# Two attention stages in one hand-ordered pipeline: the masked slots of batches 1 to 7 stand three slots later

## The chip, the cores and the metric

The kernel runs on one core of one Trainium2 chip. The metric is the device time of one execution in microseconds (us). Three runs of the kernel before gave 2798.55, 2795.04 and 2800.26 us; the median is 2798.55 us.

The engines are PE (TensorE, matmul, with its weight loads PEld), DVE (VectorE), ACT (ScalarE), POOL (GpSimd) and SP (SyncE, which issues the transfers). Each runs its own list of instructions in the order in which the kernel wrote them, and an instruction that must wait holds up what stands behind it in that list.

## The reference

`x` is 8 batches of 256 channels by 512 tokens. Four layers follow, each with a residual:

```
x = x + masked_attention(x, mask=cond)          # 8 heads of 32, keys == queries == values
x = x + modulated_attention(x, cond, ...)       # rms norm, scale and shift, 16 heads of 32, rms norm of q and k
x = x + scan_RK4(cond, drive=x)                 # 256 steps, one after another
x = x + scan_GRU(cond, inputs=x)                # 256 steps, one after another
```

Everything is float32. Only the two attention layers are touched by the change. In the masked attention, the logits of a row are `(scores * cmask + (1 - cmask) * -1e30) * rmask`, softmax over the keys, and then a 256x256 output projection. In the modulated attention, `x` is normalised per channel row, scaled and shifted by vectors made from `cond`, projected to q, k and v (512 to 1536), and attended over 256 rows in 16 heads of 32; the result is `o + o @ W_out`.

## The kernel before, in words

The function `attention` writes both attention layers for all batches as one software pipeline. Its loop `for g in range(-5, ...)` (L501) runs over **slots**; in each slot it writes a piece of several batches, in an order set by hand (`tc.manual_schedule()`, L500). Nothing reorders the instructions afterwards. A slot is only a place in this order: it has no fixed length, and lasts as long as its work and its waits.

**Masked attention of a batch** takes eight units, one for each of two groups of four heads (`e` = 0, 1) and each of four blocks of 128 keys (`kc` = 0 to 3). I write a unit as (b,e,kc). Relative to the batch's base slot, `U*b` with `U = 8`, they stand as follows.

- `load` (seven slots ahead), `project` and `mask` (L193, L208; rel. -5 and -4): the projection and its masked copy; `project_out` (L212) turns it for the values one slot later.
- `scores0` (L218; rel. -4 to 3): one unit's scores, 8 matmuls on PE into four PSUM banks, and four copies out by ACT. Then `maxima0` (L232), a 128x2048 reduction on DVE.
- `rows0` (L238; after a group's fourth maximum): PE transposes the maxima, ACT copies them (`mrow`), and two steps of transfers spread them over all partitions (`row`, then `bc`).
- `weights0` (L250; rel. 1 to 8): DVE subtracts `bc` from the unit; `exps0` (L254): ACT takes its exponential.
- `values0` (L258; rel. 2 to 9): PE sums values and weights, 16 matmuls.
- `weigh0` (L275; with a group's last `values0`): two reciprocals and two products on DVE, then two passes on POOL that make `ctxT`.
- `masked_out` (L289; rel. 10): the output projection on PE, added to `x` by DVE.

**Modulated attention of a batch**:

- `normalize` (L302; slot `norms[b]`): two squares on ACT with their sums, two tiny powers on POOL, two scaled copies `xh` on ACT. `modulate` (L314), a slot later: eight transposes and four ACT copies to `xnT`.
- `qkv` (L329), six parts, from two slots after `norms[b]` (three for batch 6), one to a slot and two to a slot for the last two batches; for q and k, `qkv_norm` (L352) on DVE and POOL and `qkv_out` (L366) a slot later.
- From `HEADS[b]` on, four groups of heads: `maxima1` (PE, DVE), `rows1`, `weights1` (PE, then ACT exponentials), `values1` (PE, DVE), one group to a slot, staggered.
- `modulated_out` (L438), in two halves, at the slots `OUT[b]`.

The order inside a slot has two forms. In a slot that is `late` (a group of heads of batch 0 to 5 is under way), `exps0` and `values0` stand at the end of the slot, and a `weigh0` that falls due is written only in the next slot, behind that slot's `maxima1` and `values1` (`due`, L513). In other slots, `values0` stands near the front and `weigh0` follows in the same slot.

PSUM gives one ring of five banks to scores, projections, transposes and outputs (`bank`, L61), used in turn, and single banks `c0`, `c1` to the two sums of `values0` and `c2` to `values1`.

In the steady state, `masked_out` of batch b stands in the slot after its last `weigh0`'s slot, and `normalize` of b one slot after `masked_out`. Behind the last output the two scans run for the rest of the span.

Of the kernel before, what the change touches and what calls it, by code (L numbers as in the profile page):

```python
# [16 lines left out]
B, T, D = 8, 256, 512  # L17
# [8 lines left out]
def attention(ctx, tc, cst, x, cond, wqT, woT, w_emb, b_emb, g_norm, w_qkv, g_q, g_k, w_out, follow):  # L26
# [21 lines left out]
    U = 8  # L48
# [12 lines left out]
    def bank(shape, name):  # L61
        return ps_s.tile(shape, F32, tag="s", name=name)
# [149 lines left out]
    def project_out(b, e, qt):  # L212
        pt = bank([P, NJ, P], f"ptq_{b}_{e}")
        for c in range(NJ):
            nc.tensor.transpose(pt[:, c, :], qt[:, c * P : (c + 1) * P], ident)
        nc.scalar.copy(qtoks[b][:, :, e * P : (e + 1) * P], pt)
# [21 lines left out]
    def rows0(b, e):  # L238

        pt = bank([P, P], f"pm0_{b}_{e}")  # L240
        nc.tensor.transpose(pt, mxp0, ident)
        mrow = ftwo.tile([P, P], F32, tag="mrow", name=f"mrow0_{b}_{e}", bufs=1)
        nc.scalar.copy(mrow, pt)
        bc = bcs[b, e] = ftwo.tile([P, 4, D], F32, tag="bc", name=f"bc_{b}_{e}")
        row = dram.tile([4, D], F32, tag="row", name=f"row_{b}_{e}", bufs=2)
        for h in range(4):
            nc.sync.dma_start(row[h].rearrange("(q n) -> q n", n=P), mrow[32 * h : 32 * h + 4, :])
        nc.sync.dma_start(bc, row.rearrange("h n -> (h n)").partition_broadcast(P).rearrange("p (h n) -> p h n", h=4))
# [126 lines left out]
    def maxima1(b, c):  # L375
        qT, kT = qTs[b], kTs[b]

        ss = []
        for h in range(4):
            n = f"n1_{b}_{c}_{h}"  # L380
            ss.append(other_bank([P, 2, 256], f"c{h}", n) if b == B - 1 and h < 2 else bank([P, 2, 256], n))
        for qc in range(2):
            for h in range(4):
                r = 32 * h
                nc.tensor.matmul(  # L385
                    ss[h][:, qc, :],
                    lhsT=qT[r : r + 32, c, qc * P : (qc + 1) * P],
                    rhs=kT[r : r + 32, c, :],
                    start=True,
                    stop=True,  # L390
                )
        for h in range(4):
            nc.vector.tensor_reduce(mxp1[:, 32 * h : 32 * h + 2], ss[h], AX.X, ALU.max)  # L393
# [36 lines left out]
    def values1(b, c):  # L430
        if c == 0:
            oTs[b] = big.tile([P, NJ, 256], F32, tag="oT", name=f"oT_{b}")
        pc = other_bank([P, 2, 256], "c2", f"pc1_{b}_{c}")
        for half in range(2):
            values(pc, half, lambda k, h: vts[b][:, k, c * P + h * DH : c * P + (h + 1) * DH], [exs1[b, c]])
        weigh(pc, oTs[b][:, c, :], f"1_{b}_{c}")
# [32 lines left out]
    PARTS = ((2, 0), (2, 1), (1, 0), (1, 1), (0, 0), (0, 1))  # L469


    norms, parts, HEADS, OUT = [], {}, [], []
    for b in range(B):
        per = 2 if b >= B - 2 else 1
        norms.append(U * b + U + (2 if b == B - 1 else 3))
        start = norms[b] + (2 if b != B - 2 else 3)
        for i, part in enumerate(PARTS):
            parts.setdefault(start + i // per, []).append((b, *part))
        HEADS.append(start + len(PARTS) // per)
        OUT.append((HEADS[b] + 6, HEADS[b] + (8 if per == 1 else 7 if b < B - 1 else 6)))  # L480

    def at(g, rel, n=1):

        b, r = divmod(g - rel, U)
        return (b, r) if 0 <= b < B and r < n else None

    def heads(g, rel, which=range(B)):

        for b in which:
            if 0 <= g - HEADS[b] - rel < NJ:  # L490
                return b, g - HEADS[b] - rel
        return None
# [3 lines left out]
    def leave(kind):  # L496
        for key in [k for k in left if k[0] == kind]:
            yield *key[1:], left.pop(key)

    with tc.manual_schedule():  # L500
        for g in range(-5, OUT[-1][1] + 1):  # L501

            a0, v0 = at(g, -4, U), at(g, 2, U)
            w1, v1 = heads(g, 1), heads(g, 2)

            a1, early = heads(g, 1, range(B - 2)), heads(g, 0, range(B - 2, B))
            late = a1 is not None or heads(g, 0, range(B - 2)) is not None
            turns, turned = list(leave("qkv")), list(leave("qt"))
            if a1:
                maxima1(*a1)  # L510
                if v1:
                    values1(*v1)
                if a := due.pop("weigh", None):  # L513
                    weigh0(*a)
            elif a0:
                scores0(a0[0], a0[1] // 4, a0[1] % 4)
            if (a := at(g, -3, U)) and a[1] % 4 == 3 and g > 0 and not a1:
                rows0(a[0], a[1] // 4)

            pr = at(g, -5, 2)  # L520
            if pr and not late:
                project(*pr)
            if v0 and not late:
                values0(v0[0], v0[1] // 4, v0[1] % 4)
            for a in turned:
                project_out(*a)
            if g == OUT[-1][1]:
                cst["soon"]()
                scan_start(cst["pool"], nc, cst)
            if g - 1 in norms:  # L530
                modulate(norms.index(g - 1))
            if a1 and a0:
                scores0(a0[0], a0[1] // 4, a0[1] % 4)
            if (a := at(g, -3, U)) and a[1] % 4 == 3 and a1:
                rows0(a[0], a[1] // 4)
            if w1:
                rows1(*w1)
            if e0 := at(g, 1, U):
                weights0(e0[0], e0[1] // 4, e0[1] % 4)
                if not late:  # L540
                    exps0(e0[0], e0[1] // 4, e0[1] % 4)
            if pr and not late:
                mask(*pr)
            if v0 and not late and v0[1] % 4 == 3:
                weigh0(v0[0], v0[1] // 4)
            if a0 and a0[1] % 4 < 3:
                maxima0(a0[0], a0[1] // 4, a0[1] % 4)

            if pr and late:
                project(*pr)  # L550
                mask(*pr)
            if a := at(g, U + 2):
                masked_out(a[0])
            if 3 <= g < 7:
                modulation(2 * g - 6)
            if g == U:
                scale_shift()
                add_identity()
            if g in norms:
                normalize(norms.index(g))  # L560
            made = [(part, qkv(*part)) for part in parts.get(g, ())]
            for b in range(B):
                for half in range(2):
                    if OUT[b][half] == g:
                        modulated_out(b, half)
                    if OUT[b][half] == g and (b, half) == (B - 1, 0):
                        for s in range(4):
                            for m in range(NJ // 2):
                                drive_of(nc, cst["us"], cst["x2T"], cst["ubias"], 0, s, m)
            if a0 and a0[1] % 4 == 3:  # L570
                maxima0(a0[0], a0[1] // 4, 3)
            if g == -1:
                rows0(0, 0)
            for part, lines in made:
                if lines:
                    qkv_norm(*part, *lines)
                    left["qkv", *part] = lines[1]
            if not w1:
                for a in turns:
                    qkv_out(*a)  # L580
            if early:
                maxima1(*early)

            if v1 and not a1:
                values1(*v1)
            if w1:
                weights1(*w1)
                for a in turns:
                    qkv_out(*a)
            if e0 and late:  # L590
                exps0(e0[0], e0[1] // 4, e0[1] % 4)
            if v0 and late:
                values0(v0[0], v0[1] // 4, v0[1] % 4)
                if v0[1] % 4 == 3:
                    due["weigh"] = v0[0], v0[1] // 4
            if (a2 := at(g, -7)) and a2[0] > 1:
                load(a2[0])
            if g == -1:
                load_weights()
            if g == U * B + 2:  # L600
                first.close()
                follow()
                for (b, half), d in x2d.items():
                    nc.sync.dma_start(
                        cst["x2T"][:, 2 * half : 2 * half + 2, b, :], d.rearrange("p (m t) -> p m t", m=2)
                    )
# [623 lines left out]
```

## Time and profile before

| what | value |
|---|---|
| three runs, median | 2798.55 us (2795.04 to 2800.26) |
| profiled execution, its own time | 2795.9 us |
| its span, first to last instruction | 2793.8 us, so 2.1 us lie around it |
| busy, share of the span | PE 96%, DVE 76%, ACT 60%, POOL 43% |
| mean granted TensorE clock | 0.988 |
| attention, by the start of the scans' matmuls | the first 826 us of the span |
| one batch in the steady state of the attention | 91.9 us |

The table is read so: the span has two parts, the attention (826 us) and the scans (the rest), and a share over the whole span says little of either. The change touches the first part alone. "Busy" on PE counts modelled ends, so PE can be busy in the profile while its matmuls stand in line for a bank.

### The profile page before, as it was taken

What the parts mean: (1) busy time and instruction counts of PE and PEld (TensorE: products, weight loads), DVE (VectorE), ACT (ScalarE), POOL (GpSimd) and SP (SyncE); (2) the same over time, 40 slices, a digit from 0 to 9 for tenths busy, and PEclk for the clock granted to TensorE, in tenths of its full rate; (3) what the DMA queues carried; (4) which work ended last, traced back from release to release, by engine and by line L of the source; (5) the groups of instructions that cost most, each with busy time, mean ns of one, the idle gap of its engine ahead of it and who ended that gap; (6) DMA issues with size and microseconds to landing.
All of it is one profiled execution on the core that took longest, in us unless ns stands there. A gap on an engine that the chain in (4) does not pass through costs nothing.

```text
span 2793.8 us, 160316 instructions
## 1 busy us (share of the span) xinstructions
PE 2684.1 (96%) x67894; PEld 1957.2 (70%) x67894; DVE 2112.7 (76%) x9216; ACT 1666.8 (60%) x8178; POOL 1210.7 (43%) x3501
## 2 busy tenths in 40 slices
PE   7799999999988999999999999999999999999998
PEld 3234445544566888888888888888888888888887
DVE  6767776775346888888888888888888888888886
ACT  5666665654336666666666666666666666666653
POOL 1144323433314444444545544544454444444443
PEclk8899999999999999999999999999999999999999
DMA  4111101100400000000000000000000000000000
GB/s 152 42 43 35 47 20 50 36 34 20 151 2 4 7 7 8 7 7 8 7 7 7 7 7 7 7 7 7 8 7 7 7 7 7 8 7 7 8 7 8
DMA packets 56785, 57.64 MB, mean 21 GB/s; under 512 B 42832, under 2 KB 46456, under 8 KB 54016
## 3 DMA queue, kind: packets, MB, share of 16 engines
q1 hardware_dynamic: 55984, 47.39, 5.3%
q8 instruction: 530, 8.68, 1.3%
q14 instruction: 191, 1.56, 0.2%
q10 hardware_dynamic: 80, 0.01, 0.0%
HBM read 40.15 MB, written 7.21 MB: 17 GB/s over the span
## 4 chain that ended last, share of the span: by engine, by line
PE 85%; ACT 6%; DVE 5%; POOL 1%; issue 1%; DMA 1%; SPq 0%; DVEq 0%; POOLq 0%; ACTq 0%
PE ic L820 34%; PE pg L853 15%; PE pn L853 8%; PE gi L835 6%; PE psqkv L334 6%; PE pc L267 3%; PE pc L177 2%; PE s L224 2%; PE psx L453 1%; PE s L407 1%; PE n L385 1%; ACT cx L791 1%; PE pso L294 1%; PE s L417 1%; ACT sc L229 1%
## 5 line engine op out<-in xcount | busy, mean ns | idle before, releaser
L820 PE MATMUL ic<-cT_sb,tT 128*8 128x128 f32 x32736 | 1084.8, 273 | 34.8 <-ACT tT L719 34.5
L820 PEld LDWEIGHTS ic<-cT_sb,tT 128*8 128x8 f32 x32736 | 757.3, 89 | 332.3 <-ACT tT L719 294.4
L719 ACT ACTIVATE tT<-qn 128x16 f32<-128x16 f32 x2046 | 440.3, 215 | 547.6 <-DVE qn L1128 457.5
L1119 DVE STREAM_TRANSPOSE icT<-ic 128x64 f32<-128x64 f32 x2048 | 504.2, 246 | 76.0 <-PE ic L820 57.4
L853 PE MATMUL pg<-whh_sb,hz 128*32 128x128 f32 x15936 | 526.3, 273 | 0.0
L815 POOL TENSOR_TENSOR W<-W,cx 128x128 f32<-128x128 f32 x765 | 298.2, 390 | 362.5 <-ACT cx L791 360.4
L853 PEld LDWEIGHTS pg<-whh_sb,hz 128*32 128x32 f32 x15936 | 445.2, 110 | 0.1
L1128 DVE SCALAR_TENSOR_TENSOR qn<-icT,hqs 128x16 f32<-128x16 f32 x2048 | 350.0, 171 | 70.1
L805 POOL TENSOR_TENSOR W<-cx,us 128x128 f32<-128x128 f32 x255 | 117.2, 460 | 484.1 <-ACT cx L791 484.1
L853 PE MATMUL pn<-whh_sb,hz 128*32 128x128 f32 x7968 | 263.1, 273 | 0.0
L853 PEld LDWEIGHTS pn<-whh_sb,hz 128*32 128x32 f32 x7968 | 222.7, 110 | 0.0
L1076 DVE SCALAR_TENSOR_TENSOR sqmm<-sqmm,qn 128x32 f32<-128x32 f32 x768 | 142.6, 186 | 98.0 <-ACT sqmm L1059 97.9
L1085 DVE TENSOR_TENSOR hqs<-W,sqmm 128x32 f32<-128x32 f32 x1020 | 195.0, 191 | 19.5 <-DVE nn L910 0.8
L835 PE MATMUL gi<-wih_sb,x3T 128*32 128x384 f32 (+2 forms) x3072 | 202.5, 381 | 0.2 <-POOL x3T L1142 0.2
L791 ACT ACTIVATE cx<-qn 128x32 f32<-128x32 f32 x1280 | 200.7, 213 | 0.0
L791 ACT ACTIVATE cx<-p 128x32 f32<-128x32 f32 x1020 | 150.0, 218 | 53.2 <-DVE p L1071 53.2
L334 PE MATMUL psqkv<-wqkv_sb,xnT 128*128 128x512 f32 x384 | 175.6, 603 | 3.8 <-ACT sc L229 3.2
L234 DVE TENSOR_REDUCE mxp<-sc 128x4 f32<-128x2048 f32 x64 | 145.9, 2281 | 26.5 <-ACT sc L229 26.2
L393 DVE TENSOR_REDUCE mxp<-n 128x2 f32<-128x512 f32 x128 | 79.4, 683 | 110.0 <-PE n L385 110.0
L229 ACT COPY sc<-s 128x512 f32<-128x512 f32 x256 | 131.4, 607 | 41.1 <-PE s L224 41.1
L252 DVE TENSOR_TENSOR sc<-sc,bc 128x2048 f32<-128x2048 f32 x64 | 147.6, 2307 | 10.7 <-DMA bc<-row 10.7
L256 ACT ACTIVATE sc<-sc,negT 128x2048 f32<-128x2048 f32 x64 | 129.0, 2018 | 34.7 <-DVE sc L252 34.7
(172 smaller groups left out, 3861.4 us busy)
## 6 DMA issues: line engine op xcount, KB each, us to landing
bc<-row SPq DMA_DIRECT2D x16, 1024.0 KB
out<-o SPq DMA_DIRECT2D x1008, 4.0 KB
x<-in_x SPq DMA_DIRECT2D x8, 512.0 KB
wqkv_sb<-in_L_cond_W_qkv SPq DMA_DIRECT2D x1, 3072.0 KB
wih_sb<-in_L_cond_W_ih SPq DMA_DIRECT2D x4, 768.0 KB
whh_sb<-in_L_cond_W_hh SPq DMA_DIRECT2D x4, 768.0 KB
x2d<-x2o SPq DMA_DIRECT2D x11, 256.0 KB
x2T<-x2d SPq DMA_DIRECT2D x11, 256.0 KB
```

What stands on the lines that cost most here:

```text
L229: nc.scalar.copy(sc[:, h, :], ss[h])
L252: nc.vector.tensor_sub(sc, sc, bcs[b, e])
L334: nc.tensor.matmul(ps, lhsT=xnTs[b][:, c, m * P : (m + 1) * P], rhs=wqkv_sb[:, c, part * D : (part + 1) * D], start=(c == 0), stop=(c == N ...
L719: seen["tanh"] = nc.scalar.activation(tT, src[:, half * HM : (half + 1) * HM, :], AF.Tanh)
L791: a = nc.scalar.activation(c[:, i], x, AF.Copy, scale=f)
L815: seen["sum"] = nc.gpsimd.tensor_tensor(W[:, i + 1 : 5], W[:, i + 1 : 5], c, ALU.add)
L820: last = nc.tensor.matmul(ps[32 * j : 32 * j + B, :], lhsT=tT[k // HM][:, k % HM, :], rhs=cT_sb[:, k, 0, :, j, :], start=(k == 0), stop=(k ...
L835: nc.tensor.matmul(gi_ps[rows(j), g0:g1, :], lhsT=x3T[c][:, k, :], rhs=wih_sb[:, k, g0:g1, :, j, :].rearrange("p g m i -> p (g m) i"), sta ...
L853: nc.tensor.matmul((pg_ps, pg_ps, pn_ps)[g][rows(j), :], lhsT=hzs[tau % 3][:, k, 32 * (g % 2) : 32 * (g % 2) + 32], rhs=whh_sb[:, k, g, :, ...
L1085: nc.vector.tensor_sub(hq, W[:, s], mm)
L1119: turn = nc.vector.transpose(icT.rearrange("p m n -> p (m n)"), ic[:, half * 64 : half * 64 + 64])
L1128: stt(qn[:, m2, :], icT[:, :, 0:B], IC[s], hq[:, m2, :], ALU.mult, ALU.add)
```

## The change

The base slot of batches 1 to 7 becomes `8*b + 3`; batch 0 stays where it is. All that is placed relative to it moves along: projections, scores, spreads, exponentials, values, `masked_out` and loads. `norms[b]` becomes `base + 10` for every batch: for batch 0 that is slot 10 (11 before), for batches 1 to 6 the same slot as `masked_out` (one slot after it before), for batch 7 as before. The parts, `HEADS` and `OUT` follow `norms`.

One block stays early: the new function `ahead` lets the unit (1,0,0) be projected in slot 3 and scored in slot 4, where they stood before, and leaves it out three slots later. So slots 5 to 7 hold no scores. `rows0(0, 1)`, the spread of the first batch's second group of maxima, moves from the front of slot 4, behind the scores of (1,0,0), to the end of slot 3, right behind its last maximum. The release of the first stage's memory and the loads of the scans' weights (`follow`) move from slot 66 to slot 69.

The number of matmuls, copies, reductions and exponentials stays the same. The whole diff:

```diff
@@ -469,10 +469,12 @@
     PARTS = ((2, 0), (2, 1), (1, 0), (1, 1), (0, 0), (0, 1))
 
 
+    LATER = 3
+    base = [U * b + (LATER if b else 0) for b in range(B)]
     norms, parts, HEADS, OUT = [], {}, [], []
     for b in range(B):
         per = 2 if b >= B - 2 else 1
-        norms.append(U * b + U + (2 if b == B - 1 else 3))
+        norms.append(base[b] + U + 2)
         start = norms[b] + (2 if b != B - 2 else 3)
         for i, part in enumerate(PARTS):
             parts.setdefault(start + i // per, []).append((b, *part))
@@ -481,8 +483,17 @@
 
     def at(g, rel, n=1):
 
-        b, r = divmod(g - rel, U)
-        return (b, r) if 0 <= b < B and r < n else None
+        for b in range(B):
+            if 0 <= g - rel - base[b] < n:
+                return b, g - rel - base[b]
+        return None
+
+    def ahead(g, rel, n):
+
+        if g - rel == U:
+            return 1, 0
+        a = at(g, rel, n)
+        return None if a == (1, 0) else a
 
     def heads(g, rel, which=range(B)):
 
@@ -500,7 +511,7 @@
     with tc.manual_schedule():
         for g in range(-5, OUT[-1][1] + 1):
 
-            a0, v0 = at(g, -4, U), at(g, 2, U)
+            a0, v0 = ahead(g, -4, U), at(g, 2, U)
             w1, v1 = heads(g, 1), heads(g, 2)
 
             a1, early = heads(g, 1, range(B - 2)), heads(g, 0, range(B - 2, B))
@@ -514,10 +525,10 @@
                     weigh0(*a)
             elif a0:
                 scores0(a0[0], a0[1] // 4, a0[1] % 4)
-            if (a := at(g, -3, U)) and a[1] % 4 == 3 and g > 0 and not a1:
+            if (a := at(g, -3, U)) and a[1] % 4 == 3 and a[0] and not a1:
                 rows0(a[0], a[1] // 4)
 
-            pr = at(g, -5, 2)
+            pr = ahead(g, -5, 2)
             if pr and not late:
                 project(*pr)
             if v0 and not late:
@@ -569,8 +580,8 @@
                                 drive_of(nc, cst["us"], cst["x2T"], cst["ubias"], 0, s, m)
             if a0 and a0[1] % 4 == 3:
                 maxima0(a0[0], a0[1] // 4, 3)
-            if g == -1:
-                rows0(0, 0)
+            if g in (-1, 3):
+                rows0(0, (g + 1) // 4)
             for part, lines in made:
                 if lines:
                     qkv_norm(*part, *lines)
@@ -597,7 +608,7 @@
                 load(a2[0])
             if g == -1:
                 load_weights()
-            if g == U * B + 2:
+            if g == U * B + 2 + LATER:
                 first.close()
                 follow()
                 for (b, half), d in x2d.items():
```

`norms` was 11, 19, 27, 35, 43, 51, 59, 66 and becomes 10, 21, 29, 37, 45, 53, 61, 69; `HEADS` was 19, 27, 35, 43, 51, 59, 65, 71 and becomes 18, 29, 37, 45, 53, 61, 67, 74. The last slot was 77 and becomes 80.

## The prediction

> **What bounds the kernel now.** I first read the busy tenths of the page, to find the stage. A slice is 69.8 us; the attention is slices 1 to 12.
>
> ```profile
> PE   7799999999988999999999999999999999999998
> DVE  6767776775346888888888888888888888888886
> PEclk8899999999999999999999999999999999999999
> ```
>
> PE is full from slice 3 on; only the first two and the last three attention slices have holes, and the clock is down in the first two. So a change of order can win PE's idle time at the start or the tail, or lose it where there is hardly any now.
>
> Next, the timeline of PE in one steady period (91.9 us: the projection at 370.29 in the chain of waits returns at 462.22). Columns here and below: start, length, engine, line, what; in brackets the idle time before and its releaser. First comes a batch's last unit of values with a part of qkv, then scores, values, and masked_out (L294).
>
> ```profile
> 424.91 1.07 PE L267 MATMUL pc<-sc,qtok 128*32 128x512 f32 x8
> 425.79 1.04 PE L267 MATMUL pc<-sc,ones 128*32 128x512 f32 x8
> 426.76 3.70 PE L334 MATMUL psqkv<-wqkv_sb,xnT 128*128 128x512 f32 x8
> ...
> 435.18 1.43 PE L224 MATMUL s<-qm 32*128 32x512 f32 x8
> 436.54 1.06 PE L267 MATMUL pc<-sc,qtok 128*32 128x512 f32 x8
> 437.42 1.04 PE L267 MATMUL pc<-sc,ones 128*32 128x512 f32 x8
> 438.39 3.70 PE L294 MATMUL pso<-ctxT,wo_sb 128*128 128x512 f32 x8
> ```
>
> From start to start a unit's scores cost 1.07, its values 1.86, a part of qkv 3.55, masked_out 3.54, half an output 4.35, a projection 1.82; a head group 1.07 (maxima), 1.87 (values), 1.97 (weights). With 8 scores and values, 6 parts, 2 halves, 2 projections, 4 head groups and the transposes a batch sums to 86.6, so 5.3 us of a period are waits. Between the last values (ended 426.8) and masked_out (438.39) lie 11.6 us of other PE work. What masked_out needs is in the timelines of DVE and POOL:
>
> ```profile
> 428.31 1.75 DVE L284 RECIPROCAL r<-pc 128x256 f32<-128x256 f32 x1
> ...
> 432.21 0.42 DVE L285 SCALAR_TENSOR_TENSOR ctxT<-r,pc 128x256 f32<-128x256 f32 x1
> ```
> ```profile
> 432.71 1.27 POOL L286 TENSOR_TENSOR ctxT<-ctxT,mk 128x512 f32<-128x512 f32 x1 [2.74 <-DVE ctxT L285]
> 434.06 1.27 POOL L287 TENSOR_TENSOR ctxT<-ctxT,fill 128x512 f32<-128x512 f32 x1
> ```
>
> DVE takes 428.31 to 432.63, POOL until 435.33: a chain of 7.0 us, hidden with 3 to spare. Last, the holes at the start:
>
> ```profile
> 58.01 2.29 DVE L252 TENSOR_TENSOR sc<-sc,bc 128x2048 f32<-128x2048 f32 x1 [3.04 <-DMA bc<-row]
> 91.97 1.94 PE L267 MATMUL pc<-sc,qtok 128*32 128x512 f32 x8 [8.69 <-DVE ctxT L285]
> 122.07 1.73 PE L267 MATMUL pc<-sc,qtok 128*32 128x512 f32 x8 [1.68 <-ACT sc L256]
> ```
>
> Here DVE bounds: 2.2 to subtract, 2.2 to find maxima, a quarter of weigh0's 4.3, so 5.5 per unit against 2.9 on PE.
>
> **The change, part by part.** No work is added; only waits can differ. I walk the new order by hand with these durations.
>
> *Start.* Until the last maximum of (0,1) (48.18) nothing differs. Its spread now goes ahead of the next scores on ACT: `mrow` ends at 49.1, not 50.93, and with the 7.1 us from there to 58.01 the subtraction starts at 56.2. SP's queue holds nothing else there, so its moved transfers cost nothing. Then weigh0(0,0) runs from 58.4 to 62.7 (64.55), which frees the two sums' banks; values (0,1,0) follow at half clock to 66.2, the modulation's matmuls and project(1,1) to 70.0, its copy on ACT ahead of the exponential of (0,1,2) (72.8), and so on to the last values of (0,1), done at 80.2. With no scores of slots 5 to 7 between, weigh0(0,1) ends at 84.5 (91.8). POOL adds 2.7: masked_out(0) starts at 87.3, and PE, whose last scores ended at 81.3, has stood 6 us by then, so half of it runs at half clock and it takes 5.3 (as the one at 712.70 does after 2.56 idle). DVE's addition ends at 93.3; squares (0.8), POOL's two powers (1.98+0.73, chain at 106.49) and `xh` (1.3) end at 98.4 (110.6 before). The first qkv starts at 102.7 instead of 126.06. That is the gain: 23.4 us.
>
> The price: norm now stands in masked_out's own slot, and its squares wait on ACT for DVE's addition. Behind them on ACT stand the copies of the scores of (1,1,0) and `mrow` of (1,0): done at 100.8, so `bc` serves at 107.8, its exponential ends at 112.1, and PE, which needs it for values (1,0,0), stands 4.8 us, restarting at half clock. The second qkv ends at 119.1. Before, at 119.6, PE had done three scores, two values, two projections, a turn and a spread more (3.21+3.72+3.64+0.59+0.3 = 11.5) and two qkv less (7.1). So the change is behind by 4.4 - 0.5 = **3.9 us**: the head start is eaten.
>
> *First period,* from there to batch 2's masked_out. Before, up to 262.0 (slot 27), PE's work sums to 126.1 of 142.4 us: 16.3 of waits. New slots 14 to 28 hold 128.7 of work. Waits: 1.7 in slots 14 to 17; in slot 18 `qkv_out` follows the last qkv with only scores between (before: scores and a projection, and still 3.58 idle at 176.79): 5.7; slots 19 and 20, where scores and head groups take turns at the five banks: 3.3. Slot 21 is the dearest. Slot 20 is late, so weigh0(1,1) is written in slot 21, behind maxima (2.4) and the values' division (2.1) on DVE, and masked_out(1) stands in that same slot: 2.4+2.1+4.3+2.7 = 11.5 us of chain against 3.3 of PE work: 8 us, 10 with the half clock. Then norm(1) holds ACT until `xh`, while the exponentials of head group 2 queue behind it and hold four banks: 3.8 in slot 22. Slots 23 to 28: 3. Sum 27.7, or **11.4 more** than before. Bounds of start and first period together (15.3): -7, if from the first qkv on waits are as before (head start 23.4 less the 16.8 of masked work left over), and +25, if each wait over 2 us restarts at half clock.
>
> *Batches 2 to 6.* Norm is a slot nearer, so masked_out comes one slot after weigh0 with only qkv, qkv_out and one scores between: 3.55+0.53+1.07 = 5.2 us of cover against 7.2 (7.0 and semaphores): PE stands 2.0. Does the clock fall? Row: after 2.22 idle the next matmuls are slow.
>
> ```profile
> 687.78 1.07 PE L267 MATMUL pc<-sc,qtok 128*32 128x512 f32 x8 [2.22 <-ACT sc L256]
> 688.66 1.66 PE L267 MATMUL pc<-sc,ones 128*32 128x512 f32 x8
> 690.25 8.17 PE L334 MATMUL psqkv<-wqkv_sb,xnT 128*128 128x512 f32 x16
> ```
>
> That costs 0.6 + 1.1 = 1.7 (1.04 and 7.03 to 7.13 at full clock); waits of 0.9 (at 416.05) cost nothing. 2.0 is nearer to the first; I take half, 0.9. The Trainium skill ("TensorE: Matmul & The Clock Gate", Part 1) drops the clock only after an idle window of about 3.4 us; by it the 0.9 would be 0, the total 4.5 lower, and the row speaks against it. Behind the addition ACT waits too: the squares, then POOL's powers (0.92, row 453.58), then `xh` at about 19 us after the slot's start; what queues there (output copy, `qkv_out`, exponential) is next needed by maxima1 at 21.9, about when PE gets there. The small bank waits before 436.54 (0.36) go. So 2.0+0.9-0.4 = 2.5 a batch, five times: **12.5**. Bounds 0 (ACT's and DVE's pause is repaid out of the 5.3) and 22 (full clock loss and 1.0 on ACT).
>
> *Tail.* masked_out(7) has 3.3 of cover against 6.8 for weigh0 and the maxima before `rows1`: 3.4 idle against 2.56 at 712.53; one spread through DRAM more, hidden: **+1**, bounds -3 and +5.
>
> Sum 3.9+11.4+12.5+1 = 28.8. On the profiled execution (2795.9) this makes 2824.7, on the median (2798.55, 2.65 higher) 2827.4; I say 2826.
>
> **Rivals.** *The head start lasts (faster).* PE is full from the first qkv on, so 23.4 earlier less 16.8 of work is 6.6 won, and if DVE and ACT have slack the 2.0 vanish among the 5.3: -6 to -12, about 2789. It decides if POOL's `ctxT` is ready within 5.2 us of the last values. For it: DVE is idle a quarter of a period. Against: weigh0 can't begin before those values end, and the rows give 7.0.
>
> *The waits trade places (no change).* The 3.9 of the start stays, slot 21's 8 us let DVE and ACT catch up so that slots 22 to 28 have none of their 6.8, and steady waits replace old ones: 3.9+11.4-6.8-3.4 (two clock losses of 1.7 that a shorter stand avoids) = 5.1: about 2803.
>
> *Every stall halves the clock (slower still).* +25, +22 and +5: 2850.
>
> **How the numbers follow.** The three runs span 5 us, so about 0.2% (5.6 us) is what a measurement of this kernel can tell from no change. The forecast gets 0.69, the dearer case 0.08, trading places 0.08, the head start 0.15. Slower 0.77, same 0.08, faster 0.15. From no change at the low end to 25+20+5 at the high one, short of all bounds at once, the range is 2799 to 2849; it leaves out the head start and little above.
>
> **What would show it.** Right: in the changed profile PE waits for `ctxT` L287 ahead of L294 about seven times, 2 us in steady periods, 6 to 8 in the first two; the period from batch 2 on is 94 to 95 us; first qkv at 102 to 105; the scans start some 29 us later and last as long as before. Wrong: a period of 92 or less, no wait ahead of L294, or a first stretch where PE's holes end before 120 us.

## The result, and the profile after

After takes **2843.64 us** (median of four runs, 2838.92 to 2844.91), before 2798.14 (four runs): a ratio of 1.0159, interval [1.0147, 1.0171], 45.5 us slower. The profiled execution of after took 2844.91 us, 49.0 above that of before, at the top of its runs; the sums below are made between the two profiled executions.

| what | before | after |
|---|---|---|
| span | 2793.8 | 2843.1 |
| mean granted TensorE clock | 0.988 | 0.978 |
| first matmul of the scans | 825.8 | 872.9 |
| scans, from there to the end | 1968.0 | 1970.2 |
| one steady period | 91.9 | 94.1 |

So 47.1 of the 49.3 us of span are lost in the attention. The busy tenths of the page of after, 71.1 us to a slice, give the places:

```profile
PE   7879899999898999999999999999999999999998
DVE  6666767776435788888788888878888887888886
PEclk8879999999989999999999999999999999999999
```

The first slice to look at is the third: before had 9 on PE and on the clock there, after has 7 and 7. This is where batch 1's `masked_out` now meets batch 0's head groups. From slice 6 to 9 PE is full and the clock is up, as before. In the twelfth, the tail of the attention, the clock is below 0.9.

**The start** went nearly as walked. In the timeline of PE (start, length, operation, in brackets the idle time before and its releaser), `masked_out(0)` waits, the first qkv starts at 103.79 and the second ends at 117.6:

```profile
89.98 4.79 PE L294 MATMUL pso<-ctxT,wo_sb 128*128 128x512 f32 x6 [5.02 <-POOL ctxT L287]
...
103.79 5.57 PE L334 MATMUL psqkv<-wqkv_sb,xnT 128*128 128x512 f32 x8
...
113.96 3.70 PE L334 MATMUL psqkv<-wqkv_sb,xnT 128*128 128x512 f32 x8
```

**Slots 19 and 20** (164.48 to 190.47) are slow without any long listed wait of PE. The granted clock, by windows of the trace (stretch, then busy time of PE, PEld, DVE, ACT, POOL, then PEclk, DMA share, GB/s):

```profile
150.00:165.00 15.00, 8.56 (x40) 2.94 (x43) 7.01 (x4) 7.74 (x10) 10.16 (x6) 0.79 0.01 1
165.00:180.00 15.00, 15.00 (x118) 8.16 (x114) 7.38 (x7) 6.64 (x11) 0.00 (x0) 0.64 0.26 105
180.00:192.00 12.00, 11.70 (x117) 5.91 (x105) 8.47 (x8) 6.18 (x10) 0.00 (x0) 0.75 0.00 1
```

The rows of PE, DVE and ACT in that stretch show who waits for whom:

```profile
159.86 1.12 PE L369 MATMUL ptqk<-ident,qr 128*128 128x128 f32 x4 [4.59 <-POOL qr L359]
...
165.99 3.35 PE L224 MATMUL s<-qm 32*128 32x512 f32 x8
...
186.90 1.94 PE L267 MATMUL pc<-sc,qtok 128*32 128x512 f32 x8
188.61 1.93 PE L267 MATMUL pc<-sc,ones 128*32 128x512 f32 x8
190.47 2.09 PE L385 MATMUL n<-kT,qT 32*128 32x256 f32 x16
```
```profile
179.50 2.48 DVE L393 TENSOR_REDUCE mxp<-n 128x2 f32<-128x512 f32 x4 [6.43 <-PE n L385]
```
```profile
182.48 2.05 ACT L229 COPY sc<-s 128x512 f32<-128x512 f32 x4 [4.83 <-PE s L224]
```

It begins with a wait of 4.59 for `qkv_out`. In finer windows the granted clock is 0.50 from 158.8 to 165.6 us, 1.00 to 169.0, 0.50 to 179.3, 1.00 to 186.1 and 0.50 to 192.9: not one long dip but three, and the second comes after a row of scores that takes 3.35 us where 1.14 is usual, which the profile counts as busy; at full clock PE must have stood for some 2 us in it. At half clock values take 1.94 and 1.93 where 1.07 and 1.04 is the length at full clock, and DVE and ACT stand for 6.43 and 4.83 us because PE is late. The mean clock of the two slots is 0.70, so of their 26.0 us some 7.8 (26.0 x 0.30) are lost clock.

**Slot 21** has the wait that the forecast put there. PE stands for 8.63 us in front of `masked_out(1)`, while DVE works off the late `weigh0` and POOL makes `ctxT`; then ACT, with the norm's squares in its list, has stood 10.99 for DVE's addition:

```profile
206.15 4.73 PE L294 MATMUL pso<-ctxT,wo_sb 128*128 128x512 f32 x6 [8.63 <-POOL ctxT L287]
```
```profile
201.01 0.42 DVE L285 SCALAR_TENSOR_TENSOR ctxT<-r,pc 128x256 f32<-128x256 f32 x1
```
```profile
204.83 1.26 POOL L287 TENSOR_TENSOR ctxT<-ctxT,fill 128x512 f32<-128x512 f32 x1
```
```profile
208.99 0.63 ACT L306 ACTIVATE xh<-x 128x512 f32<-128x512 f32 x1 [10.99 <-DVE x L297]
```

**Slot 29**, with batch 2's `masked_out`, has a short wait for `ctxT` and then a longer one that no step of the forecast named, of `qkv_out` for POOL's `qr`, with half clock behind it:

```profile
289.58 2.84 PE L294 MATMUL pso<-ctxT,wo_sb 128*128 128x512 f32 x6 [1.44 <-POOL ctxT L287]
296.05 1.11 PE L369 MATMUL ptqk<-ident,qr 128*128 128x128 f32 x4 [3.63 <-POOL qr L359]
297.09 1.94 PE L267 MATMUL pc<-sc,qtok 128*32 128x512 f32 x8
```
```profile
288.26 1.26 POOL L287 TENSOR_TENSOR ctxT<-ctxT,fill 128x512 f32<-128x512 f32 x1
289.70 2.17 POOL L357 TENSOR_SCALAR r<-s 128x16 f32<-128x16 f32 x1 [0.18 <-DVE s L355]
291.96 2.91 POOL L358 TENSOR_TENSOR r<-r,mhalf 128x16 f32<-128x16 f32 x1
294.95 1.05 POOL L359 TENSOR_TENSOR qr<-qr,r 128x512 f32<-128x512 f32 x1
```

POOL's list holds the passes for `ctxT` and right behind them the three steps of `qkv_norm`: 2.17, 2.91 and 1.05. They stood just as close in before (the pass at 434.06, the first step at 435.51), but there PE had `masked_out` and a part of qkv to do until 445.36, so that nothing waited.

**The steady period** loses its 2.2 us, but not where the forecast had it. `masked_out` has no idle time before it (384.65): two of its eight matmuls need only the first group's half of `ctxT`, and the row is 4.10 long where 3.70 is usual, so about 0.4 is lost there. The waits of PE from 300 to 680 us of after (total, times, longest) name the other place:

```profile
PE ptqk L369 <- POOL qr L359: 5.7, 4, 1.4
PE pc L267 <- ACT sc L256: 4.6, 4, 1.2
```

and the same for the equal stretch of before, 270 to 630, have no such line for `ptqk`:

```profile
PE pc L267 <- ACT sc L256: 3.6, 4, 0.9
PE psqkv L334 <- ACT sc L229: 2.6, 8, 0.5
```

So 1.4 a period goes to `qkv_out`, 0.3 to values, and most of the rest is inside the 4.10. The granted clock is 1.00 from 306 to 676 us. What holds `qkv_out` up is POOL's list again, here behind the first group's `weigh0`. After, then before:

```profile
353.38 1.27 POOL L287 TENSOR_TENSOR ctxT<-ctxT,fill 128x512 f32<-128x512 f32 x1
355.05 2.17 POOL L357 TENSOR_SCALAR r<-s 128x16 f32<-128x16 f32 x1 [0.40 <-DVE s L355]
```
```profile
402.36 1.29 POOL L287 TENSOR_TENSOR ctxT<-ctxT,fill 128x512 f32<-128x512 f32 x1
412.93 2.17 POOL L357 TENSOR_SCALAR r<-s 128x16 f32<-128x16 f32 x1 [9.28 <-DVE s L355]
```

In before 9.3 us lay between the passes for `ctxT` and the steps of `qkv_norm`; in after they follow at once.

### The profile page after: what moved, and what is told of

Read it like the earlier page. It is cut to its first block, busy times and chain, and to the rows that moved or that the text cites. A ratio compares the mean times of both kernels' runs of the same rounds, so it can differ in the third digit from the quotient of the medians.

```text
span 2843.1 us, 160309 instructions
## 1 busy us (share of the span) xinstructions
PE 2713.2 (95%) x67894; PEld 1970.9 (69%) x67894; DVE 2114.4 (74%) x9216; ACT 1669.3 (59%) x8178; POOL 1195.9 (42%) x3501
## 4 chain that ended last, share of the span: by engine, by line
PE 82%; DVE 9%; ACT 4%; POOL 3%; issue 1%; DMA 1%; SPq 0%; DVEq 0%; POOLq 0%; ACTq 0%
PE ic L831 33%; PE pg L864 15%; PE pn L864 7%; PE gi L846 6%; PE psqkv L334 4%; PE pc L267 3%; PE psx L453 2%; PE pc L177 2%; PE s L224 2%; DVE r L284 2%; PE n L385 1%; PE s L407 1%; ACT cx L802 1%; PE psq L198 1%; PE s L417 1%
## 5 line engine op out<-in xcount | busy, mean ns | idle before, releaser
L286 POOL TENSOR_TENSOR ctxT<-ctxT,mk 128x512 f32<-128x512 f32 x16 | 33.9, 2116 | 280.4 <-DVE ctxT L285 280.4
```

## The experiments

Each was compared with the kernel before on the same chip; the medians of before were 2796.57 to 2798.68. "Scans at" is the first matmul of the scans in the profiled execution (825.8 before, 872.9 after).

Single executions differ at their very start. The first transposed maxima (L241), up to which all versions are the same program, stand anywhere from 24.2 to 27.8 us, because their first rows take their usual length or about twice as long (the first scores 1.14 us in after, 2.09 in the version with the norms back). What follows is shifted with them. So for comparisons between traces I also give the stretch from these maxima to the scans, "the attention's stretch": 800.8 us before, 848.5 after, a loss of 47.7.

### The parts of the change one by one

**The norms back in their old distance**, the shift kept:

```diff
-        norms.append(base[b] + U + 2)
+        norms.append(base[b] + U + (2 if b == B - 1 else 3))
```

> Only the norms are put back to where they stood against the base (base + 11 for batches 0 to 6, base + 10 for batch 7); the three slots' shift, the early block and the early spread stay. Theory A (the loss sits in places of the order: start and first period 25 us, masked_out and qkv_out of batch 2 10 us, 2 us in each later period): from batch 2 on the order is that of before, so those 10 + 6 + 2 or more go, and slot 21 keeps its wait for POOL's ctxT of about 8 us; total 2814 to 2823 us, period 92 us. Theory B (the three slots' shift itself costs it, by a longer filling of the pipeline): 2838 to 2845.

Measured 2830.05 us, ratio 1.0114 [1.0098, 1.0129], scans at 855.5, stretch 828.5. The sooner norms cost 20.0 of the 47.7 of the stretch; most of the loss, 27.7, is the shift itself (31.4 by the medians). That lies between the two theories. The distance of modulations is 91.9 again from batch 2 on, so what is left is lost before that.

**The shift taken away**, the sooner norms kept:

```diff
-    LATER = 3
+    LATER = 0
```

> LATER = 0: no shift, but the norms a slot sooner and the early spread stay. Theory A: batch 1's masked_out and qkv_out stand as batch 2's did (about 10 us with the half clock), then 2 us in each of five periods and 2 to 4 in the tail; no slot with weigh0 and masked_out together; 2815 to 2826 us, period 94 us. Theory B: within 5 us of before, 2794 to 2803.

Measured 2814.80, at the lower end of theory A, ratio 1.0056 [1.0039, 1.0073], scans at 845.2, stretch 818.4: the sooner norms alone cost 17.6 (16.1 by the medians), and the period is 94.1. The two parts add up nearly: 17.6 + 27.7 = 45.3 against 47.7.

**The first batch's sooner spread alone**, in before:

```diff
-            if (a := at(g, -3, U)) and a[1] % 4 == 3 and g > 0 and not a1:
+            if (a := at(g, -3, U)) and a[1] % 4 == 3 and a[0] and not a1:
...
-            if g == -1:
-                rows0(0, 0)
+            if g in (-1, 3):
+                rows0(0, (g + 1) // 4)
```

> The kernel before with one edit: the spread of the first batch's second maxima stands at the end of slot 3. Theory A: bc serves 1.8 us sooner, DVE uses some of it, PE is not the bound there; -2 to +1 us, 2796 to 2800. Theory B: the same; this run is for the size of the part alone.

Measured 2798.27 (ten runs), ratio 1.0002 [0.9990, 1.0013], scans at 823.8, stretch 799.3: nothing that can be measured.

### Inside the shift: the head start

The first run leaves batch 0's norm in slot 11 while batch 1's masked work comes three slots later. The next one moves **batch 0's norm along with all others**, so that the modulated stage gets no head start:

```diff
-        norms.append(base[b] + U + 2)
+        norms.append(U * b + LATER + U + (2 if b == B - 1 else 3))
```

> x1_norms_back, but batch 0's modulated stage is three slots later too (norm in slot 14), so that from slot 12 on the order is that of before from slot 9 on, and only the thin slots 5 to 11 differ. Theory C (the first period loses because batch 0's head groups no longer alternate with batch 1's qkv, eleven slots for eight): what is left is the delay of the first values of batch 1, 92 to 112 us, so 18 to 20 us over before, 2815 to 2820. Theory D (the thin slots at the start cost nothing much, as batch 0's earlier stage repays them; later is only worse): 2830 or above.

Measured 2819.43, ratio 1.0077 [1.0062, 1.0092], scans at 843.7, stretch 816.0: theory C. Giving up the head start makes the kernel 10.6 us faster than the first run (12.5 in the stretch). In this order the head start was not only eaten, it was a loss. The waits of PE from 60 to 310 us say where. First the run with the head start (four of its lines), then the one without (three of its lines):

```profile
PE pso L294 <- POOL ctxT L287: 13.8, 2, 8.8
PE ptqk L369 <- POOL qr L359: 12.1, 4, 5.2
PE pc L267 <- ACT sc L256: 6.2, 3, 3.5
PE pc L267 <- DVE ctxT L285: 4.2, 1, 4.2
```
```profile
PE pc L267 <- ACT sc L256: 13.5, 5, 8.5
PE pso L294 <- POOL ctxT L287: 5.0, 1, 5.0
...
PE ptqk L369 <- POOL qr L359: 4.4, 2, 3.6
```

With the head start, batch 0's head groups (slots 19 to 22) run out of step with the masked work that is written beside them. `masked_out(1)` and `qkv_out` then wait for POOL, 8.8 and 7.7 us more than without it; the sum of all listed waits is 42.6 against 33.8. Without it the modulated stage and the masked stages of batches 1 to 7 stand to each other as in before, three slots later. The lag is there at batch 0's modulation (136.10 for 117.51, 18.6, of which 2.8 were there at the first maxima) and hardly changes until the scans (17.9; 15.2 in the stretch). So by its place it belongs to the start, where the three slots without scores are; these were not taken apart further.

**`masked_out(1)` alone one slot later**, on top of the first run:

```diff
-            if a := at(g, U + 2):
+            if (a := at(g, U + 2)) and a[0] != 1:
                 masked_out(a[0])
+            if g == base[1] + U + 3:
+                masked_out(1)
```

> x1_norms_back, but masked_out of batch 1 alone one slot later, out of the slot of its weigh0. Theory A: the 8.8 us wait for ctxT and the half clock of 10 us after it go; 8 to 12 us less than x1, 2818 to 2822. Theory B: masked_out now stands directly ahead of norm(1) and modulate(1), and the time comes back there; 2827 to 2833.

Measured 2826.13, ratio 1.0103 [1.0088, 1.0119], scans at 852.2, against 2830.05 without the edit. That is between the two theories, nearer to the second's end, and the intervals overlap. In the waits of 140 to 310 us the 8.8 of `masked_out(1)` are gone, but 2.1 come back at `qkv_out` (14.2 for 12.1) and 1.6 at values. The scans stand 3.3 sooner, but this execution was 2.8 ahead at the first maxima, in front of the edit: the stretch is 827.9 for 828.5. So it is not shown that the edit won anything.

**Batch 1's last `weigh0` at the end of slot 20** instead of in slot 21, in after:

```diff
-                if v0[1] % 4 == 3:
+                if v0 == (1, U - 1):
+                    weigh0(1, 1)
+                elif v0[1] % 4 == 3:
```

> The changed kernel, but batch 1's last weigh0 is written at the end of slot 20, right behind its values, instead of in slot 21 behind maxima1 and values1. Theory A: masked_out(1) waits for ctxT about 4 us instead of 8.6, and the half clock after it is shorter: 5 to 8 us less than the changed kernel, 2835 to 2839. Theory B: the wait only moves (to the maxima behind weigh0 on DVE, to ACT), 2841 to 2846.

Measured 2839.56, ratio 1.0147 [1.0132, 1.0162], scans at 868.3. The wait of 8.6 ahead of `masked_out(1)` is gone (its row at 200.14 has no idle time before it), and 2.3 come back right behind it, where a head group's matmuls wait for DVE's addition. The stretch is 842.2 for 848.5, so 6.3 of the 8.6 arrive. The time is half a us above theory A's upper end; the intervals of the two ratios overlap, so the median alone doesn't settle it. The single place is worth 4 to 6 us, not the whole loss.

### The half clock

**Throwaway matmuls in the waits of after**, written into banks that are already granted:

```diff
+    def fill(ps, n):
+        for _ in range(n):
+            nc.tensor.matmul(ps, lhsT=ident, rhs=wqkv_sb[:, 0, 0:D], start=True, stop=True)
...
+            if m == 0:
+                fill(ps, {0: 5, 1: 9, 2: 1}.get(b, 0))          # in masked_out
...
+        if (part, m) == (0, 1):
+            fill(pt.rearrange("p c t -> p (c t)"), {0: 5, 1: 4}.get(b, 0))   # in qkv_out
```

> The changed kernel with extra matmuls on PE whose results are thrown away, put where PE waits: ahead of masked_out of batches 0, 1, 2 (5, 9 and 1 of 128x128 by 128x512, 0.9 us each) and ahead of qkv_out of batches 0 and 1 (5 and 4). They add 21 us of work where PE stood 5.0 + 8.6 + 1.4 + 4.6 + 3.6 us, so the waits stay and only the granted clock changes. Theory A (the half clock after the waits is a part of the loss, some 34 us at half clock between 157 and 301 us): 8 to 16 us less than the changed kernel, 2828 to 2836. Theory B (the waits on DVE, ACT and POOL set the pace, PE's clock doesn't matter): 2840 to 2850.

Measured 2832.78, ratio 1.0122 [1.0105, 1.0139], scans at 864.7, stretch 838.6 for 848.5. Twenty-four extra matmuls of 0.46 (3.70 / 8), some 11 us of work at full clock, made the kernel 10.9 us *faster* (9.9 in the stretch), as theory A has it. The clock by windows of the trace, after and then with the fill:

```profile
150.00:175.00 25.00, 18.56 (x118) 9.27 (x121) 13.89 (x10) 11.73 (x19) 10.16 (x6) 0.74 0.06 25
175.00:200.00 25.00, 21.77 (x192) 9.42 (x184) 16.32 (x17) 11.08 (x18) 0.00 (x0) 0.77 0.11 41
```
```profile
150.00:175.00 25.00, 23.05 (x144) 10.07 (x148) 15.77 (x11) 14.98 (x21) 11.97 (x7) 0.93 0.11 38
175.00:200.00 25.00, 24.39 (x195) 12.23 (x191) 19.68 (x19) 8.48 (x16) 1.89 (x1) 0.86 0.09 28
```

So about a fifth to a quarter of the loss (9.9 of 47.7, 10.9 of 45.5) is half clock behind these waits, shown by removing it and leaving the order alone. Counted from the first maxima, the lead over after is still nothing at the front of slot 18; 2.2 come in that slot, 2.3 in slots 19 and 20 (23.7 us for 26.0), 2.7 in slot 21 and 2.9 in slot 29. In slots 19 and 20 the clock went down again (0.79 on average), with no filled wait inside them.

**The same in the version with the norms back**, at three of its waits: `{0: 5, 1: 9}` in `masked_out`, `{0: 5}` in `qkv_out`.

> After with the norms where they stood before (2830.05 by itself) and throwaway matmuls that write into banks already granted: five ahead of masked_out(0), nine ahead of masked_out(1), five ahead of one qkv_out of batch 0. Work is added, nothing is taken away. Theory C (a good part of the 10.6 us by which the version with batch 0's norm three slots nearer exceeds the one that moves all norms is matmuls at half clock behind the waits): 2820 to 2826. Rival D (the pace there is set by DVE, ACT and POOL, so a faster PE only waits longer): 2828 to 2836.

Measured 2826.51, ratio 1.0102 [1.0088, 1.0117], against 1.0114 [1.0098, 1.0129] without the fill; scans at 856.7 against 855.5, stretch 832.3 against 828.5. Time and place point to different theories (the time lies half a us above C's upper end, the stretch speaks for D), and the intervals overlap: inconclusive. The clock in 180 to 210 us rose from 0.83 to 0.89. Batch 0's modulation came 5.1 us earlier (99.79 for 104.90), half of it from the start of the execution, those of batches 1 and 2 only 0.6 (223.42 for 224.05, 304.00 for 304.61): what the first fill won was lost again on the way. So the 10.6 us of the head start are not shown to be half clock. The listed waits differ by 8.8 of them (42.6 less 33.8); the remainder stays open.

**The same in before**, with 128x128 matmuls (`ident` by `ident`) at three of its own waits:

```diff
+            hold(pt[:, 0, :], 24)     # qkv_out, batch 0, part 0, second half
...
+            hold(pt, 16)              # rows1, first group of batches 6 and 7
```

> The kernel before (not after) with throwaway 128x128 matmuls that write into banks already granted, at three of its own waits: 24 ahead of the qkv_out that waits 3.58 at 176.79, 16 each ahead of the rows1 of batches 6 and 7 that wait 2.56 at 712.53 and 2.55 at 779.69. Half clock follows each of these waits in the kernel before (granted clock 0.95, 0.90 and 0.83 in the 30 us around them). Theory C (the matmuls at half clock behind a wait are paid for in full where PE alone has work left): 2791 to 2796, with the clock in 780 to 810 us above 0.9. Rival D (other engines set the pace behind these waits, so the clock is worth nothing there): 2797 to 2802.

Measured 2795.87 against 2796.57, ratio 0.9998 [0.9989, 1.0007]: the same. At the first place the clock rose to 1.00, but the next modulation stands at 182.66 (182.77 before): nothing, as theory D has it. At the second the next one stands at 721.00 (722.98), but 1.8 of these 2.0 us were there already ahead of the place (the maxima L385 at 706.85 for 708.68). They come from the wait of 2.22 at 687.78, which nothing was written into: behind it the clock fell in before's trace and not in this one:

```profile
687.60 1.06 PE L267 MATMUL pc<-sc,qtok 128*32 128x512 f32 x8 [2.22 <-ACT sc L256]
688.48 1.04 PE L267 MATMUL pc<-sc,ones 128*32 128x512 f32 x8
```

At the third place the half clock returned some us later (0.89 in 780 to 810 us, 0.83 before). The stretch is 799.1, and 799.3 in the run with the sooner spread, which has no fill at all. So nothing is shown to be won at any of the three.

### The distance of the norm in before

**Batch 0's norm alone one slot sooner** (slot 10), in before:

```diff
-        norms.append(U * b + U + (2 if b == B - 1 else 3))
+        norms.append(U * b + U + (2 if b in (0, B - 1) else 3))
```

> The kernel before with one edit: batch 0's norm in slot 10 instead of 11 (its parts, head groups and outputs follow), no shift and the other norms as before. Theory A: xh is ready 2 to 6 us sooner, but batch 0's head groups then meet one qkv part of batch 1 less; between -4 and +4, 2795 to 2803. Theory B (a slot sooner costs in every batch alike): +2 to +3.

Measured 2807.80, ratio 1.0038 [1.0023, 1.0053], scans at 833.8, stretch 805.9: 9.8 slower by the medians, 5.1 in the stretch, more than either theory gave. Batch 0's modulation comes 7.7 us earlier (109.77 for 117.51), and batch 1's 11.8 later (194.57 for 182.77; counted from the first maxima 10.6 earlier and 8.9 later): one slot of head start is lost again, and more.

**One slot later**, for batch 0 alone, and for batches 0 to 6:

```diff
+        norms.append(U * b + U + (2 if b == B - 1 else 4 if b == 0 else 3))
```
```diff
+        norms.append(U * b + U + (2 if b == B - 1 else 4))
```

> The kernel before with batch 0's norm alone one slot later (slot 12 instead of 11; its parts, head groups and outputs follow). The same edit one slot the other way (slot 10) gave 2807.80, 9.8 slower. Theory G (the distance itself matters: each slot between masked_out(0) and its norm is cover for DVE's addition, ACT's squares and POOL's powers, and there is still waiting left in the first period): 2790 to 2796. Rival H (the cost of slot 10 came from ACT standing behind DVE's addition, which slot 11 already avoids; a further slot only starts the first qkv later): 2798 to 2806, the start of the scans' matmuls at 826 to 834 us.

> The kernel before with the norms of batches 0 to 6 one slot later (U*b + U + 4; batch 7's as before). Theory G (a slot more between masked_out and norm takes away waits in every period): period below 91.5 instead of 91.9, 2785 to 2795. Rival H (nothing waits for norm in the steady period any more, and the modulated work ends a slot later at the tail): period 91.9 to 92.1, 2799 to 2808.

The first took 2801.34, ratio 1.0011 [1.0002, 1.0019], scans at 828.9: H. The second took 2814.89, ratio 1.0056 [1.0044, 1.0069], scans at 844.0: slower than both theories had it. Its distances from one modulation to the next are 96.2, 96.3, 93.0 and 94.6 for 91.9, with the granted clock at 0.96, 0.96, 1.00 and 0.98; the listed waits are hardly longer (8.6 against 7.5 us over four periods). At those clocks the lost clock is some 3.8, 3.9, 0 and 1.9 us, so at full clock the four would be 92.4 to 93.0 us (an estimate from these figures). Why the clock is down in three of four like periods stays open. No version was found that beats before by more than the noise.

## Why the prediction was right, and where it was not

The time (2843.64) lies in the range, and slower was the likeliest sign. The sum was too small by 16.7 on the median (45.5 against 28.8), by 20.2 on the profiled executions. Term by term, in the lag at equal work, as the prediction counted it:

| term | forecast | measured | from |
|---|---|---|---|
| start | 3.9 | 2.4 | second qkv ends at 117.6, forecast 119.1 |
| first period | 11.4 | 22.5 | 285.11 - 117.6 = 167.5 to the scores ahead of `masked_out(2)`, less 128.7 of work = 38.8, which is 11.1 above the forecast 27.7 |
| batch 2's period | 2.5 | 10.0 | scores to scores 382.75 - 285.11 = 97.6 less 91.9, with one output half (4.35) fewer in it |
| batches 3 to 5 | 7.5 | 6.4 | three periods of 94.1 less 91.9 |
| batch 6, tail | 3.5 | 5.8 | the rest up to the scans, 47.1 in all |
| the scans | 0 | 2.2 | 1970.2 for 1968.0 |

*Start: right*, with errors that partly cancel: the wait ahead of `masked_out(0)` was 5.02 (forecast 6) and the first qkv at 103.8 (102.7), but that qkv took 5.57 at a lower clock, and the wait for the exponential of (1,0,0) was 1.67 (4.8). "The head start is eaten" was too kind: with the norms back, giving it up gains another 10.6.

*First period: right mechanism, mis-sized.* (Its six terms add up to 27.5, not 27.7.) Slot 21's wait was 8.63 for 8. The term that failed is slots 19 and 20: 3.3 of bank waits were allowed for, which makes about 18 us for the two with their work, and they took 26.0 (164.48 to 190.47). The wait of 4.59 ahead of them was forecast (5.7), but not that the clock would be down for more than half of the two slots, which at 0.70 on average is 7.8 us. The run with filled waits got 2.3 of them back there; the other gains of that run lie in slots 18, 21 and 29.

*Batch 2: the mis-sized term.* It was given the price of a steady period. But batch 0's second output half, which in a steady period stands between `masked_out` and `qkv_out` (388.59 in after), had already gone by (264.92), being part of the head start. So `qkv_out` met POOL's chain uncovered: 3.63, after 1.44 for `ctxT`, and half clock after that (0.52 in 295 to 302 us).

*Batches 3 to 6: right size, wrong place.* 2.15 a period for 2.5, and the period was 94.1 as forecast. But one sign that the prediction named as proof against it came true here: in these periods PE does not stand ahead of L294, and the waits for `ctxT` were three, not seven. The cover was counted too small: the first two matmuls of `masked_out` don't need the late half, and the scores ahead of it take 1.9 us from start to start (382.75 to 384.65) where 1.07 was counted. The loss is at `qkv_out`. DVE's reduction for `qkv_norm` and POOL's three steps now stand directly behind the first group's `weigh0` and its passes for `ctxT`; one slot had kept them apart. The prediction had this queue of POOL in view only for the norm's powers (0.92), not for `qkv_norm`'s 6.1. So that the period came out as forecast was in part luck: the wait that made it was another.

*The half clock per period* (0.9) was zero. Waits of 1.4 at full PE load left the clock at 1.00. The Trainium skill ("TensorE: Matmul & The Clock Gate", Part 1), which lets the clock fall only after an idle window of about 3.4 us, was right for these. The row that spoke against it, after 2.22 us of idling, is no fixed price either: with the same wait of 2.22 the clock fell in before's trace (1.66 for the next row), and stayed at 1.00 in the run with the sooner spread and in before with fills (1.04). And in slots 19 and 20 the clock fell twice more with no listed wait of even 0.5 us ahead, while the profile shows PE busy (15.00 of 15.00 at 0.64). The same page ("A second HAM failure mode: psum-queue depth-cycling") describes a clock that goes down and up when PE idles briefly between groups of matmuls as it cycles through PSUM banks. That would fit the five banks in those slots and the row of scores of 3.35; no run here varies the banks, so it isn't shown.

*Rivals.* The head start that lasts was refuted by its own condition: `ctxT` was not ready in time, and undoing the head start gains. Trading places hardly happened: taking the 8.6 us of slot 21 away brought 6.3 of them in the stretch, so most had not been repaid. The third rival, every stall halves the clock, was nearest in time (2850) but not in kind: the steady stalls halved nothing, while the stretch behind one long stall was at half clock for longer than it had allowed.

## What to carry to other kernels

In a hand-ordered pipeline of two stages, moving one stage against the other changes which pieces stand beside which: look for the piece that used to stand between a producer's last step and its consumer (here an output half ahead of `qkv_out`), because its departure can be the price. When a step is moved nearer to another, list what *both* put into the slow engine's queue, not only the step that moved. And price a long PE wait together with the stretch behind it: in after, raising the clock behind five waits won 10 to 11 us, while behind the first filled wait of before a full clock won nothing. When two single executions are compared, check first where they stand at a point ahead of the edit: here they differed there by up to 3.6 us.

## What the runs showed of the hardware

Half clock could return after the wait that began it: after 4.59 us of idling the clock was 0.50 to 165.6 us, 1.00 to 169.0 and 0.50 again to 179.3, the last with hardly any idle time in the profile. Up to the scans, every half-clock stretch in the clock records of these traces lasts a whole multiple of 3.41 us (one to six), and where the steps fall differs from execution to execution; the same wait of 2.22 us was followed by such a stretch in one and by none in another. Some 11 us of useless matmuls, put into five waits, raised the clock in 150 to 200 us from 0.74 and 0.77 to 0.93 and 0.86 and shortened the kernel by 10.9 us. The same trick in two other orders, one of them before's own, brought nothing that could be measured.
